# A graph layer on one core: edge blocks taken in pairs, b_e added by TensorE for 20 blocks, the last chunks in parts

## The chip, the cores and the metric

The kernel runs on 1 core of one Trainium2 chip. The metric is the device time of one execution in microseconds (us). Before the change it was 1358.65 us, the median of 3 runs (1356.51 to 1364.21). Times inside an execution come from one profiled execution, counted from the start of its span.

## What is computed

One layer of a graph network on 8192 nodes of 256 features and 131072 edges of 64 features, all in float32. The edges are sorted by their target node `dst`.

```python
ea = edge_attr @ w_e + b_e                              # 131072 x 256
msg = relu(x[src] + ea)                                 # rows of x gathered by src
agg = segment_sum(msg, dst, num_segments=8192)
t = x + agg
h_local = bn1(relu(t @ w1 + b1) @ w2 + b2 + x)
h_attn = bn2(attention(x in groups of 32 nodes, 4 heads) @ out_w.T + out_b + x)
out = h_local + h_attn
out = bn3(out + relu(out @ m_w1 + m_b1) @ m_w2 + m_b2)
return layernorm(x + out)
```

The three `bn` are a scale and a shift for each feature. The rows `x[src]` lie anywhere in x, so each edge fetches its own row of 1 KB.

## The kernel before, in words

**Edges.** The edges are cut into 128 blocks of 1024. A block is 4 pieces (NH) of 256 edges, and its 8 tiles of 128 edges have one edge on each partition. For a block the kernel does this:

- `gather` (L117): GpSimd (POOL) issues 8 indirect DMAs, each of which fetches 128 rows of x into the tile `xs`. It has 5 buffers of one block each.
- `load_edges` (L132): SyncE (SP) loads the features of two blocks at a time. `edge_transpose` (L414, L416): TensorE (PE) turns them, ScalarE (ACT) copies the result from PSUM.
- `edge_products` (L428 to L433): TensorE multiplies by w_e with 64 rows of its array at a time, 8 multiplications of 128x256 for a block; VectorE (DVE) adds the gathered rows (L430) and ScalarE applies relu in place (L433). The message tile `msg` has 2 buffers.
- `edge_sums` (L440 to L454): since the edges are sorted, each piece of 256 edges reaches at most 32 neighbouring target nodes (WN). A one-hot matrix made by VectorE (L440) sums the messages on TensorE into `pw` (L449), which ScalarE copies to `ws` (L454). `pw` and the turned edges share one PSUM slot.
- `edge_place` (L463 to L478): a second one-hot matrix (L463) and two multiplications (L468) move the sums of a block to their nodes; after each second block VectorE adds the result to the turned x, `xT` (L478).

**b_e.** It is added in one of two ways. For the first NX = 13 blocks the gather reads x itself, and VectorE adds b_e to the messages by a second instruction (L432). For the other blocks the gather reads `xb`, a copy of x + b_e in DRAM. `copy_x` makes that copy during the first blocks: SyncE loads 512 rows of x into `xp` (L491), VectorE adds b_e (L492), SyncE writes them to `xb` (L486). It borrows four buffers of 512 KB from tiles that later stages use.

**Nodes.** The nodes are cut into 16 chunks of 512. For each chunk `attention` and later `dense` run; they are Python generators that issue a piece of TensorE work and then yield an estimate of its time. `dense` of a chunk needs the sums of all its edges.

**The order.** TensorE runs its instructions in the order in which the program issues them. The main loop goes over the blocks. For block b it issues the load of block b+2, the gather of b+2, the products of b, then a third of the node work, the sums of b-1, another third, the turning of b+2, the last third, and the placing of b-2. `Work.run` takes pieces from two streams (attention and dense) in turn, up to an allowance of PER = 4.875 us by the estimates for each block. The other engines' orders are set by a scheduler when the program is built. Each engine waits in its order: an instruction that waits holds up all behind it. SyncE's queue holds its DMAs in the same way.

**Start and end.** Before the loop, a setup turns the index lists and the weights on TensorE, and makes the one-hot offsets on VectorE. At the end the last chunk's `dense` is issued in three parts (nodes 0 to 255, 256 to 383, 384 to 511 of the chunk), one after the other in one stream, since all three use the same buffers.

Of the kernel before, what the change touches and what calls it, by code (L numbers as in the profile page):

```python
# [9 lines left out]
FP = mybir.dt.float32  # L10
# [8 lines left out]
P = 128  # L19
# [17 lines left out]
NX = 13  # L37
ND = 2
AGG_ROWS = N + 2 * P
# [10 lines left out]
def gnn_kernel(ctx: ExitStack, tc: tile.TileContext, x, src, dst, edge_attr, w, out):  # L50
# [7 lines left out]
    nc.sync.dma_start(srcd, src[0 : ND * BE].rearrange("(g p j) -> p g j", p=P, j=TJ))  # L58
# [9 lines left out]
    nc.vector.memset(eps_t, LN_EPS)  # L68

# [37 lines left out]
    npool = fast.enter_context(tc.tile_pool(name="node", bufs=1))  # L107

# [3 lines left out]
    def gather(b):  # L112
        xs = epool.tile([P, NH, TJ, C], FP, name="xs", tag="xs", bufs=5)
# [27 lines left out]
    gather(1)  # L141

    with tc.tile_pool(name="setup", bufs=1) as sp, tc.tile_pool(name="setup_ps", bufs=4, space=PSUM) as sps:


        srci_r = npool.tile([P, BE], I32, name="srci_r", tag="y", bufs=2)
        dsti_r = npool.tile([P, BE], I32, name="dsti_r", tag="y", bufs=2)
        nc.sync.dma_start(srci_r, src.rearrange("(s e) -> s e", s=NB))
        nc.sync.dma_start(dsti_r, dst.rearrange("(s e) -> s e", s=NB))
        nc.scalar.dma_start(be, w["b_e"][None, :].to_broadcast([P, C]))  # L150
        for h in range(2):
            nc.scalar.dma_start(we[h * ED : (h + 1) * ED, :], w["w_e"])
        in_r = npool.tile([P, 3 * KC, C], FP, name="in_r", tag="m1")
        out_r = npool.tile([P, KC, C], FP, name="out_r", tag="h1")
        nc.scalar.dma_start(in_r, w["in_w"].rearrange("(o p) c -> p o c", p=P))
        vec_r = sp.tile([nrows, P], FP, name="vec_r")
        for v in VECS:
            r, n = col[v]
            nc.scalar.dma_start(vec_r[r : r + n, :], w[v].rearrange("(r p) -> r p", p=P))
        nc.scalar.dma_start(out_r, w["out_w"].rearrange("(o p) c -> p o c", p=P))  # L160
        srcf = npool.tile([P, NH, P, TJ], FP, name="srcf", tag="zT")
        nc.vector.tensor_copy(srcf.rearrange("s h p j -> s (h p j)"), srci_r)
        dstf = npool.tile([P, NH, P, TJ], FP, name="dstf", tag="y", bufs=2)
        nc.vector.tensor_copy(dstf.rearrange("s h p j -> s (h p j)"), dsti_r)
        for h in range(NH):
            ps = sps.tile([P, TJ, NB], FP, name="ps", tag="ps")
            for j in range(TJ):
                nc.tensor.transpose(ps[:, j, :], srcf[:, h, :, j], ident)
            nc.vector.tensor_copy(srci[:, :, h * TJ : (h + 1) * TJ].rearrange("p s j -> p j s"), ps)

# [6 lines left out]
        for h in range(NH):  # L177
            ps = sps.tile([P, TJ, NB], FP, name="ps", tag="ps")
# [22 lines left out]
        ps = sps.tile([P, 2, NB], FP, name="ps", tag="ps")  # L201
# [7 lines left out]


        nc.vector.memset(bd, 0.0)
        for rows, cols, no in ((in_r, inT, 3 * KC), (out_r, outT, KC)):
            for o in range(no):
                ps = sps.tile([P, KC, P], FP, name="ps", tag="ps")
                for k in range(KC):
                    nc.tensor.transpose(ps[:, k, :], rows[:, o, k * P : (k + 1) * P], ident)
                nc.scalar.copy(cols[:, :, o * P : (o + 1) * P], ps)
        ps = sps.tile([P, nrows], FP, name="ps", tag="ps")
        nc.tensor.transpose(ps, vec_r, ident[:nrows, :nrows])
        nc.vector.tensor_copy(vec, ps)  # L220

        for s, g in ((s1, "bn1_g"), (s2, "bn2_g"), (s3, "bn3_g")):
            nc.vector.tensor_scalar(s, v_(g, 0, KC), RS, None, ALU.mult)
        nc.vector.tensor_add(s12, s1, s2)
        t1 = sp.tile([P, KC], FP, name="t1")
        t2 = sp.tile([P, KC], FP, name="t2")
        nc.vector.tensor_mul(t1, s1, v_("b2", 0, KC))
        nc.vector.tensor_mul(t2, s2, v_("out_b", 0, KC))
        nc.vector.tensor_add(t1, t1, v_("bn1_b", 0, KC))
        nc.vector.tensor_add(t2, t2, v_("bn2_b", 0, KC))  # L230
        nc.vector.tensor_add(cA, t1, t2)
        t3 = sp.tile([P, KC], FP, name="t3")
        nc.vector.tensor_mul(t3, s3, v_("m_b2", 0, KC))
        nc.vector.tensor_add(c3, t3, v_("bn3_b", 0, KC))


    def attention(n0, st, pool, bank, bank2):
# [24 lines left out]
        for t0 in range(0, TN, 2):  # L262
# [10 lines left out]
            nc.vector.tensor_copy(vn[:, t0 : t0 + 2, :].rearrange("p t c -> p (t c)"), ps)  # L273
            yield 1.7

        pr = pool.tile([P, TN, H, NPG], FP, name="pr", tag="pr")
        for hh in range(H // 2):
# [15 lines left out]
            yield 0.9  # L293
# [16 lines left out]
        for k in range(KC):  # L310
# [12 lines left out]
            yield 0.9  # L323
        for o in range(KC):
# [8 lines left out]
            yield 1.7  # L333

    def dense(n0, st, pool, bank, t_a=0, t_z=TN):

        nt = t_z - t_a
# [11 lines left out]
        h1 = pool.tile([P, KC, CH], FP, name="h1", tag="h1")[:, :, : nt * P]  # L349
# [8 lines left out]
        m1 = pool.tile([P, 2 * KC, CH], FP, name="m1", tag="m1")[:, :, : nt * P]  # L358
# [3 lines left out]
        zT = pool.tile([P, KC, CH], FP, name="zT", tag="zT")[:, :, : nt * P]  # L362
# [10 lines left out]
        y = pool.tile([P, TN, C], FP, name="y", tag="y", bufs=2)[:, :nt, :]  # L373
        st6 = pool.tile([P, TN, 6], FP, name="st", tag="st")
        mv = pool.tile([P, TN, 2], FP, name="mv", tag="mv")
# [12 lines left out]
        rstd = pool.tile([P, TN], FP, name="rstd", tag="rstd")  # L388
# [7 lines left out]
        yield 0.9 * part  # L396


    pps = fast.enter_context(tc.tile_pool(name="fast_ps", bufs=1, space=PSUM))
    chunk = [{} for _ in range(NCH)]  # L400

    def bank():
# [301 lines left out]
```

## Time and profile before

| what | value |
|---|---|
| median of 3 runs | 1358.65 us |
| the profiled execution | 1364.3 us |
| its span, first to last instruction | 1362.5 us |
| TensorE (PE) busy | 1242.5 us, 91% |
| VectorE (DVE) busy | 743.0 us, 55% |
| ScalarE (ACT) busy | 662.5 us, 49% |
| 1024 gathers on GpSimd, busy | 879.3 + 98.7 + 16.5 us |
| DMA, whole span | 206.73 MB, 152 GB/s |

The span leaves out 1.8 us of the profiled execution. Busy is the share of the span in which an engine works on an instruction. A busy share is an average over stages; what sets the end is read from the waits and from the order in time. Durations in the profile are those of single instructions, and TensorE's overlap each other: for the cost of a TensorE step it is better to take the time from its start to the start of the next.

### The profile page before, as it was taken

The numbers are of one execution on the slowest core, as the hardware profiler recorded it, in microseconds if no ns is written. First come the engines' busy times: TensorE is split into PE (matmuls) and PEld (weight loads), VectorE is DVE, ScalarE is ACT, GpSimd is POOL, SyncE is SP. The second block draws the span as 40 slices with busy tenths as digits, with TensorE's granted clock in tenths as the row PEclk, the third lists the DMA queues.
The fourth block names the chain that finished last, engine by engine and source line by source line (L and its number), as shares of the span: only waits on it lengthen the run. The fifth ranks groups of instructions, "written<-read, shape, count | busy, mean of one in ns | idle before, by whom it ended". The sixth has DMA issues, their size and how long they took to land.

```text
span 1362.5 us, 20476 instructions
## 1 busy us (share of the span) xinstructions
PE 1242.5 (91%) x7939; PEld 738.2 (54%) x7939; DVE 743.0 (55%) x1218; ACT 662.5 (49%) x1014; POOL 995.5 (73%) x1032
## 2 busy tenths in 40 slices
PE   2778979899999999999999999999999999999797
PEld 2445545555556555555555555555556565565455
DVE  5687665545556463645546464555645555545452
ACT  1444444545555564545546465454645455554332
POOL 6877777777777777777777777777777777777740
PEclk9889989899999999999999999999999999999899
DMA  8994445445454454545454454544545454454421
GB/s 283 361 352 116 130 117 160 141 136 153 135 169 137 126 161 136 167 136 152 136 148 138 137 165 137 151 136 140 162 123 167 135 164 123 137 148 123 137 62 33
DMA packets 141443, 206.73 MB, mean 152 GB/s; under 512 B 19710, under 2 KB 103964, under 8 KB 141340
## 3 DMA queue, kind: packets, MB, share of 16 engines
q0 software_dynamic: 49152, 134.28, 34.6%
q1 hardware_dynamic: 90768, 69.75, 16.0%
q10 hardware_dynamic: 1420, 1.33, 0.3%
q8 instruction: 64, 1.05, 0.3%
q14 instruction: 39, 0.32, 0.1%
HBM read 188.51 MB, written 16.78 MB: 151 GB/s over the span
## 4 chain that ended last, share of the span: by engine, by line
PE 43%; POOL 23%; issue 12%; DVE 8%; DMA 8%; ACT 5%; SPq 0%; DVEq 0%; POOLq 0%; ACTq 0%
POOL xs L117 23%; PE at L344 15%; PE pe L428 8%; DMA xs<-xb,srci 6%; PE pw L449 4%; PE at L256 4%; DVE msg L430 3%; PE l L468 3%; PE at L266 2%; PE at L327 2%; PE tp L414 2%; ACT msg L433 2%; PE at L315 1%; DVE bd L307 1%; ACT pr L292 1%
## 5 line engine op out<-in xcount | busy, mean ns | idle before, releaser
L117 POOL DMA_INDIRECT xs<-xb,srci x920 | 879.3, 956 | 280.3 <-issue 264.5
L433 ACT ACTIVATE msg<-msg 128x1024 f32<-128x1024 f32 x256 | 269.4, 1056 | 361.1 <-DVE msg L430 309.7
L430 DVE TENSOR_TENSOR msg<-pe,xs 128x1024 f32<-128x1024 f32 x256 | 303.5, 1219 | 62.6 <-PE pe L428 44.0
L428 PE MATMUL pe<-we,eaT 64*128 64x256 f32 x2048 | 263.8, 397 | 1.1 <-ACT pr L292 0.8
L428 PEld LDWEIGHTS pe<-we,eaT 64*128 64x128 f32 x2048 | 190.6, 191 | 46.7 <-issue 20.2
L449 PE MATMUL pw<-msg,oh 128*32 128x256 f32 x2048 | 139.1, 390 | 0.0
L344 PE MATMUL at<-hA,mw 128*128 128x512 f32 (+2 forms) x288 | 127.8, 567 | 5.8 <-DVE hA L354 5.4
L256 PE MATMUL at<-xT,inT 128*128 128x512 f32 x256 | 126.0, 615 | 5.9 <-DVE y L384 4.0
L344 PE MATMUL at<-m,mw 128*128 128x512 f32 (+2 forms) x288 | 117.9, 554 | 6.6 <-ACT xT L246 6.5
L117 POOL DMA_INDIRECT xs<-in_x_dram,srci x88 | 98.7, 1121 | 26.8 <-issue 26.2
L416 ACT COPY eaT<-tp 128x512 f32<-128x512 f32 x128 | 74.5, 582 | 86.7 <-PE tp L414 86.1
L414 PE MATMUL tp<-ident,ea 128*128 128x128 f32 x512 | 81.4, 282 | 35.4 <-ACT ws L454 32.4
L414 PEld LDWEIGHTS tp<-ident,ea 128*128 128x128 f32 x512 | 60.6, 143 | 92.4 <-ACT ws L454 56.6
L449 PEld LDWEIGHTS pw<-msg,oh 128*32 128x32 f32 x2048 | 54.0, 110 | 100.6 <-issue 45.0
L468 PEld LDWEIGHTS l<-oh,ws 128*128 128x128 f32 x512 | 82.3, 195 | 39.5 <-issue 36.9
L440 DVE TENSOR_TENSOR oh<-iota_n,rel 128x256 f32<-128x256 f32 x128 | 54.1, 423 | 75.7 <-PE pw L449 75.6
L468 PE MATMUL l<-oh,ws 128*128 128x160 f32 x512 | 94.2, 308 | 0.5 <-ACT ws L454 0.5
L369 DVE SCALAR_TENSOR_TENSOR zT<-at,s,zT 128x512 f32<-128x512 f32 (+2 forms) x36 | 24.9, 692 | 123.4 <-PE at L344 122.1
L463 DVE TENSOR_SCALAR oh<-iota_n,wrow 128x160 f32<-128x160 f32 x128 | 41.6, 325 | 84.9 <-PE l L468 84.8
L344 PEld LDWEIGHTS at<-m,mw 128*128 128x128 f32 x288 | 49.9, 190 | 57.9 <-issue 45.8
L478 DVE TENSOR_TENSOR xT<-l,xT 128x352 f32<-128x352 f32 (+3 forms) x95 | 42.2, 464 | 62.6 <-PE l L468 62.4
L344 PEld LDWEIGHTS at<-hA,mw 128*128 128x128 f32 x288 | 47.5, 190 | 50.4 <-issue 34.1
(106 smaller groups left out, 1313.8 us busy)
## 6 DMA issues: line engine op xcount, KB each, us to landing
ea<-in_edge_attr_dram SPq DMA_DIRECT2D x64, 512.0 KB, 4.5
xs<-xb,srci POOLq DMA_INDIRECT x920
xn<-in_x_dram SPq DMA_DIRECT2D x16, 512.0 KB, 5.0
xp<-in_x_dram SPq DMA_DIRECT2D x16, 512.0 KB, 6.5
xb<-xp SPq DMA_DIRECT2D x16, 512.0 KB
out_dram<-y SPq DMA_DIRECT2D x15, 512.0 KB, 3.2
xs<-in_x_dram,srci POOLq DMA_INDIRECT x88
mw<-in_L_gnn_m_w_dram SPq DMA_DIRECT2D x2, 512.0 KB
```

Of the source, the lines that this page charges most:

```text
L117: nc.gpsimd.indirect_dma_start(out=xs[:, h, j, :], out_offset=None, in_=x if b < NX else xb[:, :], in_offset=bass.IndirectOffsetOnAxis(ap= ...
L256: nc.tensor.matmul(ps, inT[:, k, o * P : (o + 1) * P], xT[:, k, :], start=(k == 0), stop=(k == KC - 1))
L344: nc.tensor.matmul(ps, wt[:, k, o * P : (o + 1) * P], act[:, k, :], start=(k == 0), stop=(k == nk - 1))
L414: nc.tensor.transpose(tp[:, h, :], ea[:, h, :], ident)
L416: nc.scalar.copy(eaT, tp)
L428: nc.tensor.matmul(pe[:, i, u, :], eaT[rows, h + u, :], we[rows, :], start=True, stop=True)
L430: nc.vector.tensor_add(half, pe, xs[:, h : h + 2].rearrange("p u i c -> p i u c"))
L433: nc.scalar.activation(msg[:, h : h + 2], msg[:, h : h + 2], AF.Relu)
L440: nc.vector.tensor_tensor(oh, iota_n[:, None, :WN].to_broadcast([P, TB, WN]), rel[:, b, :, None].to_broadcast([P, TB, WN]), ALU.is_equal,)
L449: nc.tensor.matmul(pw[h * WN : (h + 1) * WN, :], oh[:, h * TJ + j, :], msg[:, h, j, :], start=(j == 0), stop=(j == TJ - 1),)
L468: nc.tensor.matmul(l2[:, k, odd * NPB : odd * NPB + WB], ws[:, k * P : (k + 1) * P], oh2, start=(not odd and k == 0), stop=bool(odd or alo ...
L478: nc.vector.tensor_add(xT, l2[:, :, a - n : z - n], xT)
```

## The change

The blocks are taken by pairs up to block 117 and one by one for the last 10 (NS). For a pair (b, b+1) the program issues: the products of b, the sums of the pair before (both blocks), the products of b+1, half of the pair's node work, the one-hot matrices of the pair, the turning of b+2, the placing of the pair before, the turning of b+3, the other half of the node work.

- b_e is added on TensorE for the first 20 blocks (NX), by as many multiplications again as the products: the rows of `sel` that pick one row of `be`. VectorE's second add is gone.
- `copy_x` moves 256 rows at a time (XH) through two buffers of its own, and is called for 16 blocks instead of 8; the add of b_e stands just ahead of the write.
- `xs` has 4 buffers instead of 5, `msg` 3 instead of 2.
- The setup turns the edges of blocks 0 and 1 first, then the source indices and the weights, then the target indices; the small vectors are loaded on SyncE's queue. It uses the loop's PSUM buffers.
- `dense` of the last two chunks is issued in parts (two of chunk 14, three of chunk 15), each as soon as its sums are placed; three of the parts use buffers of the attention stage (OTHER) and run in the other stream. In the last 10 blocks the allowance of node work is 1.3 times as large.

```diff
-NX = 13
+NX = 20
+NS = 10
+XH = 256
...
-        xs = epool.tile([P, NH, TJ, C], FP, name="xs", tag="xs", bufs=5)
+        xs = epool.tile([P, NH, TJ, C], FP, name="xs", tag="xs", bufs=4)
...
-            nc.scalar.dma_start(vec_r[r : r + n, :], w[v].rearrange("(r p) -> r p", p=P))
+            nc.sync.dma_start(vec_r[r : r + n, :], w[v].rearrange("(r p) -> r p", p=P))
...
-            half = msg[:, h : h + 2].rearrange("p u i c -> p i u c")
-            nc.vector.tensor_add(half, pe, xs[:, h : h + 2].rearrange("p u i c -> p i u c"))
             if b < NX:
-                nc.vector.tensor_add(half, half, be[:, None, None, :].to_broadcast([P, 2, 2, C]))
-            nc.scalar.activation(msg[:, h : h + 2], msg[:, h : h + 2], AF.Relu)
+                for u in range(2):
+                    for i in range(2):
+                        rows = slice(i * ED, (i + 1) * ED)
+                        nc.tensor.matmul(
+                            pe[:, i, u, :], sel[rows, :], be[rows, :], start=False, stop=True, skip_group_check=True
+                        )
+            n = 2 if b < NB - 1 else 1
+            for u in range(0, 2, n):
+                hs = slice(h + u, h + u + n)
+                nc.vector.tensor_add(
+                    msg[:, hs].rearrange("p u i c -> p i u c"), pe[:, :, u : u + n, :],
+                    xs[:, hs].rearrange("p u i c -> p i u c"),
+                )
+                nc.scalar.activation(msg[:, hs], msg[:, hs], AF.Relu)
...
+        for c in range(k * i - k, k * i):
+            if 0 <= c < N // XH:
+                xp = xp_of.pop(c)
+                nc.vector.tensor_add(xp, xp, be[:, None, :].to_broadcast([P, XH // P, C]))
+                nc.sync.dma_start(xb[c * XH : (c + 1) * XH, :].rearrange("(p t) c -> p t c", p=P), xp)
+        for c in range(k * i, k * i + k):
+            if c < N // XH:
+                xp = xp_of[c] = epool.tile([P, XH // P, C], FP, name="xp", tag="xp", bufs=2)
+                nc.sync.dma_start(xp, x[c * XH : (c + 1) * XH, :].rearrange("(p t) c -> p t c", p=P))
...
+    parts = [
+        (NCH - 2, 0, 2, OTHER), (NCH - 2, 2, 4, None), (NCH - 1, 0, 2, OTHER), (NCH - 1, 2, 3, None),
+        (NCH - 1, 3, 4, OTHER),
+    ]
...
+            edge_products(b)
+            sums = edge_sums(waiting) if waiting else None
+            waiting = list(blocks)
+            if n == 2:
+                edge_products(b + 1)
+            work.run(n * per / 2)
+            if n == 2:
+                copy_x(b + 1)
+            for i in blocks:
+                edge_hot(i)
+            for i in blocks:
+                if i + 2 < NB:
+                    edge_transpose(i + 2)
+                if sums:
+                    place(sums)
+                    sums = None
+            if b < NB - 1:
+                work.run(n * per / 2)
+            b += n
+        work.run(2.0)
+        sums = edge_sums(waiting)
+        work.run(1.0)
+        place(sums)
         work.finish()
```

## The prediction

> **What bounds the kernel now.** I read the page first (busy shares, granted clock, the costly groups), then the waits, then GpSimd's gathers by stretches of time, then the timeline near block 12 and at the end.
>
> ```profile
> PE 1242.5 (91%) x7939; PEld 738.2 (54%) x7939; DVE 743.0 (55%) x1218; ACT 662.5 (49%) x1014; POOL 995.5 (73%) x1032
> ...
> L117 POOL DMA_INDIRECT xs<-xb,srci x920 | 879.3, 956 | 280.3 <-issue 264.5
> ...
> out_dram<-y SPq DMA_DIRECT2D x15, 512.0 KB, 3.2
> ```
>
> ```profile
> POOL xs L117 <- issue: 295.2, 969, 0.3
> ```
>
> ```profile
> 50.00:100.00 50.00, 40.11 (x33) 0.90 1.02 363
> ...
> 500.00:600.00 100.00, 75.77 (x80) 1.00 0.49 142
> ```
>
> The page alone says TensorE, at 91%. The waits correct it: GpSimd's idle time is 0.3 us of issue ahead of nearly every gather, never longer. So its 73% are a full queue: a gather takes 0.947 + 0.303 = 1.25 us, 80 per 100 us, 10.0 us a block (the second stretch above; the columns are GpSimd's busy time and count, clock, DMA share, GB/s). From 50 to 100 us there are only 33 in 50 us, while the DMA engines are saturated by the copy of x (share 1.02).
>
> ```profile
> 6.16 1.10 POOL L117 DMA_INDIRECT xs<-in_x_dram,srcd  x1 [4.56 <-DMA srcd<-in_src_dram]
> ...
> 188.34 1.23 DVE L430 TENSOR_TENSOR msg<-pe,xs 128x1024 f32<-128x1024 f32 x1 [0.17 <-PE pe L428]
> ...
> 1311.40 0.95 POOL L117 DMA_INDIRECT xs<-xb,srci  x1 [0.30 <-issue]
> ```
>
> The gathers run from 6.2 to 1312.4 us: 1306 us, of which 1024 x 1.25 = 1280 are the floor and 26 are slow gathers early on. The add at 188.34 belongs to block 12, whose gathers were issued by 152.8: TensorE runs some 35 us behind GpSimd there, and catches up to about 4 us by the end. So the time is: 6 (start) + 1280 + 26 + 50 after the last gather = 1362.5.
>
> ```profile
> 1347.41 1.39 PE L344 MATMUL at<-xT,w 128*128 128x128 f32 x8
> ...
> 1357.54 0.41 DVE L392 TENSOR_SCALAR y<-y,mv,rstd 128x256 f32<-128x256 f32 x1
> ```
>
> This is the last of the three parts of chunk 15 that run one after the other, 10.5 us by itself.
>
> **The change part by part.** Only three terms can move: the start, what GpSimd loses against its floor (26 us now), and the 50 us behind it.
>
> *Parts at the end.* Now the sums of block 127 start at 1326.9, 7 us after its last relu, behind older node work, and the third part starts 20 us later still, behind the other two. After: in the last 10 blocks TensorE may do 1.3 x 4.875 = 6.3 us of estimated node work per block; the estimates add up to 630 us in all and the allowances to 638, so only what has to wait for the last sums remains. Counted from the last gather: the adds of block 127 end at +5; its sums follow behind the last piece at +10, placing at +12, the add to xT at +13; the part of 128 nodes 10.5 as above, and 2 for the other part that interleaves with it, gives +25.5; from the last VectorE instruction to the end of the span 4.5 (1362.5 - 1358.0). Sum 30 instead of 50: **-20**. Bounds: -14 (blocks of 11 us of TensorE work leave it 6 us behind) to -24.
>
> *b_e on TensorE.* The same multiplications as the products; start to start those take 1.93 us:
>
> ```profile
> 1297.16 2.00 PE L428 MATMUL pe<-we,eaT 64*128 64x256 f32 x16
> 1299.09 1.98 PE L344 MATMUL at<-hA,mw 128*128 128x512 f32 x4
> ```
>
> 20 blocks x 1.93 = 39 us more on TensorE. What goes is VectorE's 26 second adds of 1.22 (32 us), which were off the path except that relu waited for them. From 197 to 1132 us TensorE is busy 901 us for 96 blocks, 9.4 a block. So blocks 8 to 19 need 9.4 + 1.9 = 11.3 where GpSimd needs 10: it falls back further.
>
> *Four xs buffers.* The gather of block g+4 must wait until the adds of block g are done. On GpSimd's floor the gather of block g+4 starts at 6 + 10(g+4). With five buffers TensorE's lag of 35 us never held GpSimd (no such wait in the list); with four, a lag over 30 us does, and what is lost is not won back, since GpSimd has no slack. So GpSimd's loss is the largest value of (end of block g's adds) - 46 - 10g. Slow gathers ahead of that point are absorbed by it, not added: the 26 now go.
>
> *The copy through two small buffers.* This sets when block 8 is added. In the changed program's order of instructions all 32 adds of b_e to `xp` stand on VectorE ahead of block 8's first add to messages. Each has to wait for a load, and each load for the write two tiles before: 16 rounds of load, add, write, one after the other. Behind a waiting `xp` add stand VectorE's message adds, and TensorE behind those for its PSUM; behind the waiting load on SyncE's queue stand the edge loads. The trace has no 256 KB round through one buffer. Nearest rows: a 256 KB write lands in 2.1 us (the DMA list's row of one such output), a 256 KB load in the crowded start in 4.9 (`out_r`), 512 KB loads in 4.5 to 5.0 and writes in 3.2. Lower end: load 2.6 (half of 512 KB's moving time saved), add 0.7, issue and wakes 0.5, write 2.1: 5.9. Upper end: load 4.9, two adds, write 3.2, issues: 9.9. The Trainium skill ("DMA: Bandwidth & Descriptors", section Bandwidth) speaks against this edit: batch DMAs to 1 MiB or more, below that the fixed part rules; its fit for the other descriptor path, 2.0 us + bytes/436e3 (section on the anatomy of a DMA), gives 2.6 for each transfer and an estimate of 6.4 for a round. I take **7.0**, nearer to the lower rows since this copy asks 512 KB each way in 7 us, 150 GB/s with 105 for gathers and some 40 for other loads, under the 363 of the saturated stretch; the rule's round would make the end 9 us earlier.
> First xp add at about 31 us (26.4 now; the vectors now stand ahead of it on SyncE's queue), the last at 31 + 15 x 7 = 136, block 8's adds done at 34 + 105 = **139**. Without the copy TensorE would be there at about 120 (products of block 0 at 36 instead of 41, since no xp add stalls the setup; eight blocks of about 10; some idle time), so the copy decides.
>
> *Then* block 20's adds are done at 139 + 12 x 11.3 = 275. GpSimd's loss: 275 - 46 - 200 = **29**, against 26 now: **+3**. With a round of R us it is 15R - 76. By the clock the term could be larger: from 100 to 200 us the granted clock is 0.91 now, and the skill ("TensorE: Matmul & The Clock Gate", Part 1) says that an idle window of about 3.4 us halves the clock. By that row 12 blocks could cost 10 us more; by the rule, TensorE without such idle windows runs at full speed, as at 400 to 600 us here (1.00). I take the rule's case, because from block 8 on TensorE has work waiting.
>
> *Pairs.* Fewer waits for the shared PSUM slot (TensorE's turning waits 32 us in all for `ws` now). After block 20 TensorE needs 9.4 a block or less against 10.0, so nothing of this reaches the end: worth **0**, hidden by GpSimd. If pairs made TensorE slower than 10.0, each 0.1 would cost 11 us over 108 blocks. I see no such wait: sums, placing and transposes each have other work between them and what they need, and the third msg buffer covers the pair.
>
> *Setup.* First gather at 6 as now; the source indices must be turned by 26 us, when the 16 gathers that need no turning are issued; now that is at 16.7, and a second edge load ahead of them adds 2: **0**. If late by 5, it is absorbed by the loss at block 20.
>
> Sum: 1362.5 - 20 + 3 - 1 (rounding of the terms) = 1344.5 for the span; the profiled execution, 1364.3, would be 1346. It lies 5.6 above the median of the runs; 1358.65 - 18 gives **1341**.
>
> **The rivals.**
> - *The copy is slower* (R of 9 or more, with the loads queueing behind writes on SyncE): loss 15 x 9 - 76 = 59, +33 - 20 = +13: 1372. This is the slower case. It decides from R = 8.7 (+27.6 - 20 = over +6.8). For it: two buffers, strict order on two queues, DMAs 4 times longer in the crowded stretch (11.2 at most). Against it: the rows of 2.1 and 3.2.
> - *Nothing measurable*: R of 7.8 to 8.7, or the late start of the last parts eats the gain: 1358.
> - *The copy hardly holds* (R = 6): block 8 at 124, loss 14, -12 - 20: 1327. For it: the lower rows.
> - *Pairs stall TensorE*: 10.2 a block after block 20 gives +22, 1363; against it 9.4.
>
> **How the numbers follow.** About 0.5% is what a measurement of this kernel can tell from no change: 6.8 us. The likeliest, 1341: 0.42; the quick copy, 1327: 0.22; nothing measurable, 0.17; the slow copy 0.13 and stalls of the pairs 0.06 end slower or just above no change. Faster 0.64, same 0.18, slower 0.18. The range: R = 6 with the best end (-36) gives 1322, taken down to 1319 for the start; above, R = 8.7 with the weak end (-14) is +13.6, 1366 with something taken off for both together. The likeliest case's own range is 1330 to 1351.
>
> **What would show it.** In the profile after: the gathers' first wait for `msg` adds (four buffers), and where; the last xp add near 136 and block 8's adds near 139; the last gather near 1315; 30 us behind it. Wrong would be: gathers that are held after block 20, an end behind the last gather of over 40 us, or a granted clock of 0.9 from 140 to 280 us.

## The result, and the profile after

The changed kernel takes 1405.01 us (median of 4 runs, 1400.7 to 1409.8); the kernel before takes 1358.2 (median of 4). Ratio 1.034, 95% interval 1.029 to 1.039: slower by about 46 us, where 18 faster was forecast. The profiled execution took 1402.89 us, its span is 1401.1, against 1362.5 before.

The page after, with the rows that answer to those of before:

```profile
PE 1259.7 (90%) x8307; PEld 791.2 (56%) x8307; DVE 711.8 (51%) x1222; ACT 667.6 (48%) x966; POOL 981.4 (70%) x1032
...
L134 POOL DMA_INDIRECT xs<-xb,srci x864 | 824.1, 954 | 267.9 <-issue 249.5
...
L134 POOL DMA_INDIRECT xs<-in_x_dram,srci x144 | 140.0, 972 | 84.4 <-DVE msg L465 42.9
...
out_dram<-y SPq DMA_DIRECT2D x14, 512.0 KB
```

TensorE's share is 90% where it was 91%, so busy shares tell nothing. What is new is the idle time before the gathers of the first blocks: 42.9 us of it end with an addition to messages. The waits after:

```profile
POOL xs L134 <- issue: 293.0, 962, 0.3
...
DVE xp L527 <- DMA xp<-in_x_dram: 67.3, 26, 6.4
...
POOL xs L134 <- DVE msg L465: 51.9, 22, 14.4
...
PE at L384 <- DVE hA L394: 28.0, 8, 4.5
```

Three waits are new or much longer: GpSimd for free xs buffers (51.9 us, as four buffers made one expect), VectorE for the loads of the copy (67.3; 15.7 before), and TensorE for a vector step inside `dense` (28.0; 5.4 before). Where the time lies is seen when the span is cut at the first product of blocks 20 and 118 (L451 in the timeline after, L428 before):

| stretch | before, us | after, us | difference |
|---|---|---|---|
| start to block 20 | 261.8 | 287.4 | +25.6 |
| block 20 to block 118 | 962.4 | 976.7 | +14.3 |
| block 118 to the end | 138.3 | 137.0 | -1.3 |
| span | 1362.5 | 1401.1 | +38.6 |

The last gather ends at 1340.4 us, 60.7 ahead of the end (before: 1312.3 and 50.2), and the last additions to messages come 36.2 us behind it (before 6.4): at the end GpSimd no longer sets the pace, TensorE is late. From the last additions to the end it is 24.5 us.

**The first stretch.** TensorE from the first product of block 0 to that of block 20, first before, then after (columns: length, busy time and count of PE, PEld, DVE, ACT, POOL, then clock, DMA share, GB/s):

```profile
40.80:261.80 221.00, 186.02 (x1225) 115.25 (x1224) 147.57 (x194) 99.68 (x157) 171.12 (x163) 0.92 0.61 192
```

```profile
31.10:287.40 256.30, 212.97 (x1497) 145.00 (x1496) 117.24 (x178) 97.41 (x141) 162.47 (x170) 0.92 0.60 182
```

TensorE is busy 27.0 us longer and idle 43.3 us in place of 35.0; the first product comes 9.7 us sooner. 27.0 + 8.3 - 9.7 = 25.6. What TensorE's idle time waits for shows on VectorE, here in the changed kernel from 48 to 72 us:

```profile
48.88 0.69 DVE L527 TENSOR_TENSOR xp<-xp,be 128x512 f32<-128x512 f32 x1 [4.89 <-DMA xp<-in_x_dram]
50.86 0.69 DVE L527 TENSOR_TENSOR xp<-xp,be 128x512 f32<-128x512 f32 x1 [1.28 <-DMA xp<-in_x_dram]
56.94 0.69 DVE L527 TENSOR_TENSOR xp<-xp,be 128x512 f32<-128x512 f32 x1 [5.38 <-DMA xp<-in_x_dram]
61.54 0.69 DVE L527 TENSOR_TENSOR xp<-xp,be 128x512 f32<-128x512 f32 x1 [3.91 <-DMA xp<-in_x_dram]
62.15 1.28 DVE L310 COPY vn<-at 128x512 f32<-128x512 f32 x2
68.08 0.69 DVE L527 TENSOR_TENSOR xp<-xp,be 128x512 f32<-128x512 f32 x1 [4.65 <-DMA xp<-in_x_dram]
69.61 0.69 DVE L527 TENSOR_TENSOR xp<-xp,be 128x512 f32<-128x512 f32 x1 [0.84 <-DMA xp<-in_x_dram]
70.22 2.35 DVE L465 TENSOR_TENSOR msg<-pe,xs 128x1024 f32<-128x1024 f32 x2
```

VectorE spends these 21 us on six additions of the copy, each of which waits for its load; the next additions to messages start at 70.22.

**The second stretch.** The same 400 us before and after:

```profile
851.00:1251.00 400.00, 379.55 (x2452) 221.16 (x2450) 211.83 (x351) 207.03 (x310) 303.31 (x318) 1.00 0.50 143
```

```profile
851.00:1251.00 400.00, 360.74 (x2328) 216.06 (x2324) 201.84 (x339) 198.12 (x274) 303.45 (x318) 0.96 0.49 142
```

GpSimd issues 318 gathers in both. TensorE does less after (2328 instructions in place of 2452), is idle 39 us in place of 20, and its clock is 0.96 in place of 1.00. Two of the gaps on TensorE, then VectorE ahead of the second:

```profile
1032.30 2.84 PE L384 MATMUL at<-hA,mw 128*128 128x512 f32 x6 [3.29 <-DVE hA L394]
...
1107.42 1.99 PE L384 MATMUL at<-h,w 128*128 128x512 f32 x4
1109.24 1.02 PE L384 MATMUL at<-hA,mw 128*128 128x512 f32 x2
1113.54 5.49 PE L384 MATMUL at<-hA,mw 128*128 128x512 f32 x6 [3.29 <-DVE hA L394]
```

```profile
1109.04 1.22 DVE L465 TENSOR_TENSOR msg<-pe,xs 128x1024 f32<-128x1024 f32 x1
1110.18 0.69 DVE L345 STREAM_TRANSPOSE bd<-pr 32x512 f32<-32x512 f32 x1
1110.80 1.17 DVE L465 TENSOR_TENSOR msg<-pe,xs 128x1024 f32<-128x1024 f32 x1
1112.00 0.70 DVE L345 STREAM_TRANSPOSE bd<-pr 32x512 f32<-32x512 f32 x1
1112.74 0.75 DVE L394 SCALAR_TENSOR_TENSOR hA<-at,s,hA 128x512 f32<-128x512 f32 x1
```

At the second gap the layer of w2 (h by w) ends at 1109.4; the layer of m_w1 (hA by mw), which reads its result, is issued right behind it, with no edge work between. VectorE's update of hA stands behind messages and transposes of the softmax and starts at 1112.74. TensorE idles 3.29 us, and the six multiplications behind the gap take 5.49 us. Behind the first gap, of the same length and kind, the same six took 2.84 us; the last section comes back to this. Between 849 and 1264 us such waits for hA come 5 times (18.5 us of the 39.3 us of idle time there).

### The profile page after: what moved, and what is told of

Same layout as the page of the kernel before. It is cut to its first block, busy times and chain, and to the rows that moved or that the text cites. A ratio compares the mean times of both kernels' runs of the same rounds, so it can differ in the third digit from the quotient of the medians.

```text
span 1401.1 us, 21219 instructions
## 1 busy us (share of the span) xinstructions
PE 1259.7 (90%) x8307; PEld 791.2 (56%) x8307; DVE 711.8 (51%) x1222; ACT 667.6 (48%) x966; POOL 981.4 (70%) x1032
## 4 chain that ended last, share of the span: by engine, by line
PE 42%; POOL 19%; DMA 12%; issue 10%; DVE 10%; ACT 6%; DVEq 0%; ACTq 0%; POOLq 0%; SPq 0%
POOL xs L134 19%; PE at L384 14%; PE pe L451 8%; DMA xs<-xb,srci 4%; DVE msg L465 4%; PE pw L489 4%; PE at L293 4%; DMA xb<-xp 3%; DMA xp<-in_x_dram 3%; PE l L507 3%; PE at L365 2%; PE tp L167 2%; PE at L303 2%; DVE bd L345 1%; ACT pr L330 1%
## 5 line engine op out<-in xcount | busy, mean ns | idle before, releaser
L134 POOL DMA_INDIRECT xs<-xb,srci x864 | 824.1, 954 | 267.9 <-issue 249.5
L469 ACT ACTIVATE msg<-msg 128x1024 f32<-128x1024 f32 (+1 forms) x258 | 270.5, 1049 | 356.9 <-DVE msg L465 351.2
L465 DVE TENSOR_TENSOR msg<-pe,xs 128x1024 f32<-128x1024 f32 (+1 forms) x258 | 304.2, 1209 | 112.5 <-PE pe L451 76.8
L451 PE MATMUL pe<-we,eaT 64*128 64x256 f32 x2048 | 265.2, 394 | 23.9 <-DVE msg L465 18.8
L451 PEld LDWEIGHTS pe<-we,eaT 64*128 64x128 f32 x2048 | 188.7, 189 | 108.2 <-issue 39.7
L134 POOL DMA_INDIRECT xs<-in_x_dram,srci x144 | 140.0, 972 | 84.4 <-DVE msg L465 42.9
L293 PE MATMUL at<-xT,inT 128*128 128x512 f32 x256 | 124.6, 627 | 10.4 <-ACT qk L296 3.8
L489 PE MATMUL pw<-msg,oh 128*32 128x256 f32 x2048 | 125.0, 383 | 0.0
L517 DVE TENSOR_TENSOR xT<-l,xT 128x352 f32<-128x352 f32 (+4 forms) x99 | 43.3, 463 | 142.2 <-PE l L507 141.9
L384 PEld LDWEIGHTS at<-hA,mw 128*128 128x128 f32 x304 | 54.9, 199 | 92.4 <-issue 41.5
L507 PE MATMUL l<-oh,ws 128*128 128x160 f32 x512 | 84.6, 308 | 1.1 <-ACT ws L495 1.1
L293 PEld LDWEIGHTS at<-xT,inT 128*128 128x128 f32 x256 | 47.3, 198 | 64.9 <-issue 42.6
L365 PE MATMUL at<-oT,outT 128*128 128x512 f32 x128 | 63.6, 622 | 10.2 <-ACT oT L360 7.8
```

What stands on the lines that cost most here:

```text
L134: nc.gpsimd.indirect_dma_start(out=xs[:, h, j, :], out_offset=None, in_=x if b < NX else xb[:, :], in_offset=bass.IndirectOffsetOnAxis(ap= ...
L293: nc.tensor.matmul(ps, inT[:, k, o * P : (o + 1) * P], xT[:, k, :], start=(k == 0), stop=(k == KC - 1))
L365: nc.tensor.matmul(ps, outT[:, k, o * P : (o + 1) * P], oT[:, k, :], start=(k == 0), stop=(k == KC - 1))
L384: nc.tensor.matmul(ps, wt[:, k, o * P : (o + 1) * P], act[:, k, :], start=(k == 0), stop=(k == nk - 1))
L451: nc.tensor.matmul(pe[:, i, u, :], eaT[rows, h + u, :], we[rows, :], start=(b >= NX or u == 0), stop=(b >= NX), skip_group_check=True,)
L465: nc.vector.tensor_add(msg[:, hs].rearrange("p u i c -> p i u c"), pe[:, :, u : u + n, :], xs[:, hs].rearrange("p u i c -> p i u c"),)
```

## The experiments

Each row cuts the span of the profiled execution as above, in us; the ratio is of run times, each to the kernel before that ran beside it. "e9_no_be", "e9_no_copy_add" and "e8_data" leave out or change part of the computation.

| kernel | to 20 | 20 to 118 | 118 to end | span | ratio to before (95%) |
|---|---|---|---|---|---|
| before | 261.8 | 962.4 | 138.3 | 1362.5 | 1 |
| after | 287.4 | 976.7 | 137.0 | 1401.1 | 1.034 (1.029 to 1.039) |
| e1_copy4 | 279.1 | 977.9 | 137.1 | 1394.1 | 1.024 (1.022 to 1.026) |
| e2_be_vector | 251.9 | 988.5 | 139.1 | 1379.5 | 1.013 (1.011 to 1.015) |
| e9_no_be | 251.8 | 980.0 | 139.8 | 1371.6 | 1.009 (1.005 to 1.013) |
| e9_no_copy_add | 269.9 | 976.7 | 137.0 | 1383.6 | 1.020 (1.016 to 1.023) |
| e9_single4 | 292.0 | 965.5 | 132.7 | 1390.2 | 1.023 (1.020 to 1.027) |
| e3_phase | 292.2 | 1004.2 | 127.1 | 1423.5 | 1.044 (1.042 to 1.046) |
| e5_single | 286.3 | 963.4 | 136.7 | 1386.4 | 1.022 (1.019 to 1.026) |
| e8_hold | 288.5 | 963.0 | 134.6 | 1386.1 | 1.021 (1.017 to 1.024) |
| e8_data | 286.2 | 969.7 | 136.4 | 1392.3 | 1.025 (1.020 to 1.029) |
| e4_allow1 | 286.1 | 977.8 | 129.4 | 1393.3 | 1.028 (1.023 to 1.033) |
| e7_before_parts | 263.8 | 962.6 | 130.6 | 1357.0 | 0.994 (0.993 to 0.996) |
| e10_parts_order | 263.3 | 962.2 | 130.4 | 1355.9 | 0.996 (0.995 to 0.997) |
| e12_be_rest | 256.7 | 970.1 | 135.8 | 1362.6 | 1.002 (1.001 to 1.003) |
| e12_be_rest_single | 253.2 | 972.7 | 130.9 | 1356.8 | 0.996 (0.994 to 0.998) |

### The front: the copy, or b_e on TensorE?

**e1_copy4**, the changed kernel with four copy buffers, two of them borrowed from `dense`:

```diff
-                xp = xp_of[c] = epool.tile([P, XH // P, C], FP, name="xp", tag="xp", bufs=2)
+                tag = ("xp", "h1", "xp", "zT")[c % 4] if c < 22 else "xp"
...
```

> The changed kernel with four buffers for the copy of x instead of two (two of them borrowed from the dense stage until tile 22). Theory that the rounds of the copy set the early stage and TensorE then paces the rest: the last xp add falls from 153 to about 115, the products of block 20 start at about 255 to 265 instead of 287, and the end moves by as much, to a span of about 1375. Rival, that GpSimd's gathers set the end and TensorE is only late: the last gather moves from 1340 to about 1315 and the end moves by the same 25 us, but only if TensorE's lag at the end stays 33 us. If the copy is not the cause, the products of block 20 stay at 287 and the span at 1401.

The last xp addition came at 125.7 us in place of 152.8, so a round took 6.4 us in place of 8.2. But block 8's first product came only 8 us sooner (146.2 for 154.0), and the end 7 us sooner. The pace of the copy alone does not set the front. (The edit also moved the copy's additions further ahead in VectorE's queue: all 32 stand ahead of block 6's additions to messages, in the changed kernel ahead of block 8's.)

**e2_be_vector**, b_e by VectorE's second addition again, without the products with `sel`:

```diff
-                            pe[:, i, u, :], sel[rows, :], be[rows, :], start=False, stop=True, skip_group_check=True
...
+                if b < NX:
+                    half = msg[:, hs].rearrange("p u i c -> p i u c")
+                    nc.vector.tensor_add(half, half, be[:, None, None, :].to_broadcast([P, 2, n, C]))
```

> The changed kernel with b_e added by VectorE's second add for the 20 blocks, as the kernel before did it for 13, and no b_e multiplications. TensorE has 39 us less to do in blocks 0 to 19. If the copy holds those blocks until block 8, only 12 x 1.9 = 23 us of them can show: products of block 20 at about 265 instead of 287, span about 1380. If the b_e multiplications are all hidden behind the copy, 287 and 1401 stay. If VectorE's extra 40 x 1.2 us stands in the way of the copy's adds, block 8 gets later than 154.

Block 20 came at 251.9 us, 35.5 sooner; 21.6 of that were left at the end of the span. The copy was not quicker: its last addition came at 200.3, because the scheduler now put copy additions further back in VectorE's queue (18 of the 32 ahead of block 8's additions to messages). So this run moves two things at once; the next two were made to part them.

**e9_no_be**, no b_e in the first 20 blocks at all (those messages lack it):

```diff
-                            pe[:, i, u, :], sel[rows, :], be[rows, :], start=False, stop=True, skip_group_check=True
...
```

> The changed kernel without any b_e in the messages of the first 20 blocks (no products with the selection matrix; those messages lack b_e, so the output isn't the reference's); the copy with b_e for the later blocks stays. Theory A (the delay of 25.6 us at block 20 against the kernel before is the price of the 16 extra products a block, about 1.9 us each block of TensorE): block 8's first product comes at 139 us in place of 154, block 20's at 250 to 255 in place of 287. Rival B (the copy's additions, which wait for their loads in VectorE's queue with the message additions behind them, set the first eight blocks, whatever TensorE has to do): block 8 stays within 5 us of 154, and block 20 comes at 262 to 268.

Block 20 at 251.8, the same as with 40 additions more on VectorE: at block 20 b_e on VectorE costs nothing, and taking it off TensorE saves 35.6 us. The row for this stretch:

```profile
31.70:251.80 220.10, 178.76 (x1178) 111.67 (x1177) 114.50 (x178) 96.42 (x141) 161.35 (x166) 0.93 0.68 208
```

TensorE is busy 178.8 us in place of 213.0, a difference of 34.2, and idle 41.3 in place of 43.3. It looks as if the added work was paid and nothing else changed. Cut at block 8 it looks otherwise, first the changed kernel, then e9_no_be:

```profile
31.10:154.00 122.90, 86.25 (x577) 60.49 (x577) 52.66 (x75) 37.98 (x58) 70.14 (x73) 0.83 0.76 238
154.00:287.40 133.40, 126.72 (x921) 84.50 (x920) 64.58 (x105) 59.43 (x83) 92.33 (x98) 1.00 0.45 130
```

```profile
31.70:117.40 85.70, 64.31 (x449) 41.90 (x448) 43.06 (x60) 37.46 (x58) 65.29 (x68) 0.94 0.84 260
117.40:251.80 134.40, 114.45 (x730) 69.78 (x729) 71.45 (x119) 58.97 (x83) 96.06 (x99) 0.92 0.58 175
```

The whole difference lies ahead of block 8, where the changed kernel takes 37.2 us longer: TensorE is busy 22 us more, at a clock of 0.83 in place of 0.94, and idle 15 us more. Behind block 8 both take the same time: there the products add 12 us of busy time, and the idle time is 13 us less (6.7 for 20.0). So the two idle times agree by chance. This run does not part the two things either: the copy's additions moved here too (23 of the 32 stand ahead of block 8's additions, and the last came at 170.7 in place of 152.8). How much of the 37 us is the price of the products, and how much comes from that order, stays open. Block 8's time of 117 us lies below both theories.

**e9_no_copy_add**, the copy without its additions (messages from block 20 on lack b_e), the products with `sel` kept:

```diff
-                nc.vector.tensor_add(xp, xp, be[:, None, :].to_broadcast([P, XH // P, C]))
```

> The changed kernel without the additions of b_e in the copy: each half chunk of x is loaded and written on as it is (messages from block 20 on lack b_e, so the output isn't the reference's). The DMAs are the same; VectorE's queue no longer holds 32 additions that wait for loads (67.3 us of waits). Theory A (TensorE's extra products set the front): block 8 within 6 us of 154 us, block 20 within 6 us of 287. Rival B (message additions stuck behind the copy's additions set the first eight blocks): block 8 at 120 to 130 us, block 20 at 255 to 262.

Block 8 came at 111.1 us, 43 sooner: message additions stuck behind copy additions did hold the first blocks, as B said (its times, 120 to 130 and 255 to 262, were both missed). TensorE had the products to do here and still came to block 8 earlier than in e9_no_be. But of the 43 us only 17.5 were left at block 20. TensorE, and below it SyncE's queue:

```profile
121.05 1.03 PE L459 MATMUL pe<-be,sel 64*128 64x256 f32 x8
146.27 1.09 PE L167 MATMUL tp<-ident,ea 128*128 128x128 f32 x4 [24.19 <-DMA ea<-in_edge_attr_dram]
```

```profile
99.71 0.43 SPq L149 DMA_DIRECT2D ea<-in_edge_attr_dram  x1
...
127.65 2.46 SPq L527 DMA_DIRECT2D xb<-xp  x2
131.08 2.21 SPq L531 DMA_DIRECT2D xp<-in_x_dram  x2
134.93 2.85 SPq L527 DMA_DIRECT2D xb<-xp  x2
138.61 0.33 SPq L531 DMA_DIRECT2D xp<-in_x_dram  x1
138.99 0.45 SPq L149 DMA_DIRECT2D ea<-in_edge_attr_dram  x1
```

The next edge load stands behind the copy's loads and writes on SyncE, leaves at 138.99, and TensorE waits 24.19 us for it. One queue was freed, and the other that the copy runs through took over.

**e9_single4**, single blocks from block 4 on:

```diff
-            n = 2 if b < NB - NS else 1
+            n = 2 if b < 4 else 1
...
-            per = PER if n == 2 else 1.3 * PER
+            per = PER if b < NB - NS else 1.3 * PER
```

> The changed kernel with pairs only for the first 4 blocks and single blocks from there, so that beside the run with singles from block 20 on it tells what pairs do between blocks 4 and 20. If pairs are no part of the delay at the front: block 20's first product within 5 us of the 286 us of that run, span 1386 within 6. If two blocks' products ahead of each other's additions do hold TensorE there: block 20 at 265 to 275 and the span 10 us or more below 1386.

Block 20 at 292.0, 5.7 us later than in e5_single (below), which has pairs there. Pairs are not what costs at the front.

### The middle: why TensorE is slow behind block 78

From block 78 to 118 a block takes 10.38 us after and 9.92 before, where the gathers ask for 10.0; between 20 and 78 the changed kernel took 9.68, as it caught up with the gathers.

**e3_phase**, a slightly larger allowance of node work, which shifts the pieces against the blocks:

```diff
-    PER = 39.0 / BPC
+    PER = 39.4 / BPC
```

> The changed kernel with one number different: the allowance of node work for 8 blocks is 39.4 instead of 39.0 us, just the sum of the estimates of one chunk, so that the pieces keep the place against the pairs that they have at blocks 20 to 50. Theory that the pieces drift until two dependent pieces of the dense stage stand next to each other without cover: TensorE's time per block from 78 to 118 falls from 10.4 to about 9.7 us, the lag at the end falls by 25 us, the span to about 1376. Rival, that pairs become slow late for another reason (GpSimd's gathers arriving just in time, contention): 10.4 stays and the span stays within 5 us of 1401.

My direction was wrong: the stretch grew by 27.5 us, and blocks 40 to 60 took 10.29 us each instead of 9.42. TensorE's idle time moved to other neighbours (34.6 us of waits for ScalarE's `h`, 30.1 for its `qk`). What it shows is that TensorE's rate depends on which pieces come to lie side by side.

**e5_single**, pairs only up to block 20 (the allowance as in e9_single4):

```diff
-            n = 2 if b < NB - NS else 1
+            n = 2 if b < 20 else 1
```

> The changed kernel with pairs only up to block 20 and single blocks behind it, so that one block's sums, and runs of node work half as long, stand between the products. Theory A (what slows TensorE behind block 78 is node work in long runs, in which a layer follows at once on the layer whose output VectorE has yet to write): the gaps ahead of m_w1's products (28.0 us in all in the changed kernel, 8 of them) fall to 15 or less, the rate between blocks 78 and 118 goes from 10.4 us a block to 9.8, and the span falls by 15 to 25 us, to about 1380. Rival B (the sums and products of two blocks in one visit are not to blame, and what was lost ahead of block 20 is simply carried to the end): the rate stays at 10.4 and the span within 6 us of 1401.

963.4 us for the stretch, 13 less; the waits of m_w1 on hA fell from 28.0 to 14.3, and the rate from 78 to 118 came to 9.88. Single blocks have runs of node work half as long. This speaks for A, but pairs and long runs went together here.

**e8_hold**, pairs kept, and a rest between w2's and m_w1's layers:

```diff
+HOLD = LATER - 1
...
+        yield HOLD
         m1 = pool.tile([P, 2 * KC, nt * P], FP, name="m1", tag=own[1])
...
+                elif t == HOLD:
+                    self.rest[ready[0]] = 1
```

> The changed kernel, in which a dense stage that has issued its w2 layer rests until the next run of node work, so that m_w1's products never follow at once on the w2 products on which VectorE's update of hA still has to be made. Nothing else is changed. Theory A (that adjacency costs 18.5 us of idle TensorE between blocks 78 and 118, and more through the halved clock behind each gap): the waits of m_w1's products on hA fall from 28.0 us to under 8, the rate from 78 to 118 from 10.4 to 9.8 us a block, the last adds' lag behind the gathers from 36 to about 15 us, the span to about 1380. Rival B (the gaps only stand in for work that is late anyway; another wait takes their place): the gaps go, the rate stays above 10.2 and the span within 6 us of 1401.

963.0 us, 13.7 less, with pairs kept. No wait of m_w1 on hA is left in the list, the rate from 78 to 118 is 10.0, the pace of the gathers. The row of the same 400 us:

```profile
851.00:1251.00 400.00, 369.17 (x2421) 223.13 (x2420) 209.87 (x348) 205.88 (x289) 303.25 (x318) 0.98 0.49 143
```

The clock is at 0.98 in place of 0.96, and 93 TensorE instructions more are done. The last additions came 13.7 us behind the last gather in place of 36.2. So what A forecast for the waits and the lag came, and the rate came to the gathers' pace. My 1380 was too low by 6: the work left behind the last additions grew by 7 (31.9 for 24.5). One thing is not excluded: the rest also shifts all later pieces, and a mere shift moved this stretch by 27.5 us in e3_phase. A rest at another place was not run.

**e8_data**, m_w1's products on another tile that is long ready (the MLP's input is left out of the sum):

```diff
-            nc.scalar.activation(m1[:, o, :], layer(mw1, KC, o, hA), AF.Relu, bias=v_("m_b1", o))
+            nc.scalar.activation(m1[:, o, :], layer(mw1, KC, o, tT), AF.Relu, bias=v_("m_b1", o))
```

> The changed kernel with m_w1's products reading the x tile in place of hA: the same products in the same order, but the output isn't the reference's, as the MLP's input is left out of the sum. No product waits any more for VectorE's update of hA. Theory A: as with the rest between the layers, the waits on hA at m_w1 go (28.0 us to 0), the rate from block 78 to 118 comes to 9.8 us a block or less, and the span to about 1375 to 1385. Rival B (another wait takes the gaps' place): rate above 10.2, span within 6 us of 1401.

Only half came: 969.7 us, and 10.22 a block from 78 to 118. Of the waits for the same step of VectorE 11.5 us were left (4 times). The code gives the likely reason: the layers write into PSUM tiles `at`, of which there are two, and the second output of m_w1 needs the one that the update of hA has yet to read. In the trace m_w1 runs four multiplications ahead of its wait, where the changed kernel runs two, and then waits for L394 (2.43 us at 1108.00). So the edit took the data away and left the buffer; my "no product waits any more" was wrong, and this run tests less than it was meant to. Products of q and k also waited longer for VectorE's `y` (10.7 us, up to 3.7 each, all between blocks 20 and 78), as B would have it.

### The end: parts and allowance

**e7_before_parts**, the kernel before with the parts, the second set of buffers and the allowance of 1.3 in the last 10 blocks:

```diff
+            per = PER if b < NB - NS else 1.3 * PER
...
+                    d = dense(c * CH, chunk[c], npool, bank, t_a, t_z, *([own] if own else []))
+                    work.add(0 if own else 1, d)
```

> The kernel before with one part of the change alone: the last two chunks' dense stage in five parts on two buffer sets and two streams, and 1.3 times the node work in the last 10 blocks. No pairs, b_e and copy as before, five xs buffers. If the parts are worth what was forecast, the last gather stays at 1312 and what lies behind it falls from 50 to about 30 us: span about 1342, 1.5% faster than before. If the larger allowance makes TensorE fall behind GpSimd, as it does in the changed kernel (12.0 us a block in the last nine), the lag at block 127 grows from 6 to 15 or more and the span is 1350 to 1362.

A gain of 7.7 us from block 118 on (130.6 for 138.3), 0.6% of the time, where 20 were forecast.

**e4_allow1**, the changed kernel without the larger allowance:

```diff
-            per = PER if n == 2 else 1.3 * PER
+            per = PER
```

> The changed kernel with the ordinary allowance of node work (4.9 us a block, where the change has 6.3) in the last 10 blocks. In the changed kernel those blocks go at 11.9 to 12.2 us each with TensorE about 94% busy. Theory A (a backlog of node work is worked off in these blocks because the larger allowance lets it in): blocks 118 to 127 go at 10.3 or less, so the last product starts some 15 us sooner, but the work left then stands behind the last placement: the stretch after the last adds grows from 24.5 us to 35 to 40, and the end is within 6 us of the changed kernel's 1401 us span. Rival B (the single blocks themselves, not the node work, are slower): blocks 118 to 127 stay at about 12 us and the end doesn't move or gets later by 10.

Blocks 118 to 127 took 9.8 us each in place of 12.0 and the last product came 20 us sooner, but 12 of them came back behind it (41.3 us from the last product's start to the end for 29.4). A was right that this is a trade of one for the other, and low on what stays: 7.8 us of the span, where within 6 was expected (by the ratios, 1.028 and 1.034, the two intervals overlap).

**e10_parts_order**, e7 with 1.5 times the allowance and the last block's sums ahead of the remaining node work:

```diff
-            per = PER if b < NB - NS else 1.3 * PER
+            per = PER if b < NB - NS else (1.5 * PER if b < NB - 1 else 2.0)
...
-            if b < NB:
+            if b < NB - 1:
```

> The kernel before with the last chunks in parts and two buffer sets (1357 us, 0.994 of the kernel before) and two further edits: 7.3 us of node work a block in the last 10 blocks in place of 6.3, and almost none between the last block's products and its sums, so that the sums and the placement of block 127 stand ahead of the work that is left. If the last placement sets the end: it comes at 1324 us in place of 1335, and with 22 us behind it the span is about 1346 to 1350. Rival: TensorE was busy without a gap from 1317 to 1350 us, so the order doesn't matter, only the amount: span within 3 us of 1357.

The rival was right. The last placement came 10.8 us sooner than in e7, the last step of the output only 1.1. First e7, then e10:

```profile
1334.70 0.81 PE L468 MATMUL l<-oh,ws 128*128 128x160 f32 x4 [0.55 <-ACT ws L454]
```

```profile
1352.04 0.41 DVE L392 TENSOR_SCALAR y<-y,mv,rstd 128x256 f32<-128x256 f32 x1
```

```profile
1323.92 0.81 PE L468 MATMUL l<-oh,ws 128*128 128x160 f32 x4 [0.55 <-ACT ws L454]
```

```profile
1350.90 0.41 DVE L392 TENSOR_SCALAR y<-y,mv,rstd 128x256 f32<-128x256 f32 x1
```

Here it is the amount of work left that counts at the end; its order hardly does.

### Both causes away

**e12_be_rest** joins e2 and e8_hold; **e12_be_rest_single** adds single blocks from 20 on. The same two kernels also ran on another chip, where the kernel before took 1916 us: 2004 us (ratio 1.049) and 1902 us (0.992). There the profile has long waits whose cause it cannot name (165 us on ScalarE in the one, 227 in the other), so the argument does not rest on these.

> The changed kernel with b_e by VectorE's second addition in the first 20 blocks and the rest between w2 and m_w1; pairs, half-chunk copies, four xs buffers and parts stay. If the two causes are the whole loss and add up: block 20 at 252 us, the loss of the gathers 33 us in place of 57, the last adds some 14 us behind the last gather, span 1386 - 24 = 1362, to 1357 if TensorE keeps up all the way. If something else in the change still costs: 1370 or more, with a rate above 10.2 us a block somewhere behind block 20. If it beats before's 1358.5 us clearly (under 1352), the parts' gain of about 20 us comes through as I forecast it.

> As the run beside it, with single blocks from block 20 on. If pairs cost something of themselves once the layers no longer adjoin: 8 us or more below that run, about 1350. If they don't: within 5 us of it.

1363.97 us (span 1362.6), as forecast for two causes that add up: the kernel is back at before's time, not below. This is not all that the change costs, though: against e7, which has the new end alone, block 20 comes 7 us sooner, but the middle and the end take 13 us more. Which part of the change costs this is open. With single blocks 1356.27 us, 7.7 less. This is not a better rate in the middle (972.7 for 970.1); it comes 3.5 us ahead of block 20, where the two programs issue the same work, and 4.9 behind block 118. What pairs as such cost stays open at this size, between the 5 and the 8 us that were to decide it; on the other chip the single blocks took 5% less. e12_be_rest_single, e7 and e10 are the only ones below before, by 0.4 to 0.6%, and their intervals do not put one of them first.

## Why the prediction was wrong

Forecast for the span: -20 (parts) + 3 (front) + 0 (pairs). Measured, by the three stretches: -1.3, +25.6, +14.3.

*"The copy decides" block 8, and the loss is +3.* This step failed, in two terms. Block 8's additions to messages end at 162.9 us in the changed kernel, at 131.2 in e9_no_be and at 119.4 in e9_no_copy_add:

```profile
160.54 2.35 DVE L465 TENSOR_TENSOR msg<-pe,xs 128x1024 f32<-128x1024 f32 x2
```

```profile
130.03 1.16 DVE L458 TENSOR_TENSOR msg<-pe,xs 128x1024 f32<-128x1024 f32 x1
```

```profile
117.07 2.36 DVE L465 TENSOR_TENSOR msg<-pe,xs 128x1024 f32<-128x1024 f32 x2
```

The first term is the hold of the copy. Without its additions 119.4 us is what the forecast had (120); with them it was to be 139 and was 162.9, so the hold cost 43 us in place of 19. A round took 8.2 us in place of 7.0 (the rule's estimate of 6.4 was further off), which is 18 of the 24 us; most of the rest is that the additions of block 8 ended 10 us behind the copy's last, not 3. The forecast took its round from loads of 4.5 to 5.0 us of other tiles; the same list of the kernel before has the copy's own loads:

```profile
xp<-in_x_dram SPq DMA_DIRECT2D x16, 512.0 KB, 6.5
```

The second term is the products with `sel`, which were charged nothing ahead of block 8, as hidden behind the copy. Without them block 8's additions ended 31.7 us sooner although the copy was still there. So forecast and kernel differ in kind: the copy's hold and TensorE's work were taken as alternatives of which the later counts, and taking away either one moved block 8 by 32 to 43 us. (In e9_no_be part of this may be the changed order of the copy's additions.) At block 20 the price was 35.6 us.

Behind block 8 the forecast was right: 11.1 us a block for 11.3. Block 20's additions end at 291.0, which makes the loss 291.0 - 46 - 200 = 45 in place of 29. With the measured round, 15R - 76 gives 47, but e1 shows that this agreement is by chance: at R = 6.4 the formula says 20, and 36.6 was measured.

*Four buffers.* The mechanism was right: GpSimd waited for message additions, 51.9 us in all, 12 times for longer than the ordinary 0.3 us of issue, between 73 and 314 us. It hands on TensorE's lateness: with b_e on VectorE (e2) no such wait is longer than 0.3 us. What a fifth buffer would have saved in the changed kernel was not run.

*The clock.* Between blocks 8 and 20 it was right: 1.00 from 154 us on, the rule's case. Ahead of block 8 it was 0.83, which the forecast had not priced, and behind block 78 0.96, through gaps that I had not seen.

*Pairs: "worth 0, hidden by GpSimd... I see no such wait".* This step failed. TensorE's need of 9.4 a block or less was right (busy 9.2 from block 20 to 78, 9.4 from 78 to 118); it was wrong that only work counts. 0.6 us a block of slack has to hold all waits as well: behind block 78 they were 39.3 us, 0.98 a block. The longer runs of node work put w2's layer and m_w1's side by side. The rival "pairs stall TensorE at 10.2", to which I gave 0.06, is what happened behind block 78 at 10.4. Its name was wrong: with the rest (e8_hold) pairs reach 10.0.

*Parts: -20.* This term was mis-sized. The 30 us from the last gather assumed that only the work of the last sums remains. From the last additions to the end the forecast was right (24.5 for 25), but only because TensorE had come late: in blocks 118 to 127 it did the backlog at 12 us a block. With TensorE on time (e7) 37.5 us remain behind the last additions. What was too small is the work that has to wait for the last two chunks; the sum of estimates (630 against 638) does not say when a piece becomes free to be done. The gain was 8 us in e7.

## What to carry to other kernels

When one engine is nearly as full as the one that paces, count its waits with its work: 9.4 us of work in 10.0 leave 0.6 for every wait, and taking off it again the 1.9 us a block of 20 blocks brought back 35.6 us at block 20. When independent work is merged into longer runs, look at which dependent steps become neighbours; a rest of one run between them brought back 14 us here. Before charging a step as hidden, name the idle time that is to hide it, and cut the stretch where the limits change: behind block 8 the run without the products was idle for about as long as they take, ahead of block 8 they came on top of the waits.

## What had not been expected of the hardware

A gap of 3.29 us in TensorE's work can cost more than itself. The clock around the gap that ends at 1113.54, in the changed kernel (it stands behind the counts of the five engines):

```profile
1109.30:1112.70 3.40, 0.96 (x3) 0.13 (x1) 3.37 (x4) 1.75 (x2) 2.52 (x3) 1.00 0.38 108
1112.70:1119.50 6.80, 5.96 (x10) 2.76 (x11) 2.17 (x4) 2.29 (x4) 5.24 (x6) 0.50 0.35 101
1119.50:1125.00 5.50, 5.50 (x23) 3.37 (x22) 1.05 (x3) 2.33 (x5) 4.21 (x5) 0.99 0.63 188
```

The clock halves while the gap still lasts and stays so for 6.8 us. TensorE works 5.96 us of them, so some 3.0 us are lost on top of 3.29 (an estimate: half of 5.96). Length alone does not decide it. Behind the other gap of 3.29 us, which ends at 1032.30, the clock stays at 1.00 and the six multiplications take 2.84 us instead of 5.49; a gap of 2.29 us that ends at 783.91 is followed by 3.4 us at 0.50. By the traces' records of the clock there are 9 such stretches of 3.4 or 6.8 us between blocks 20 and 118 in the changed kernel, 44 us in all, and 2 before, 7 us in all.

The Trainium skill ("TensorE: Matmul & The Clock Gate", Part 1) says this of idle windows of about 3.4 us that run free of the program. The lengths of the stretches agree with that, and a window that runs free of the program would explain why gaps of one length have two outcomes. But the window need not be idle throughout: in the 3.4 us ahead of 1112.7 TensorE still worked 0.96. I had cited the rule for the start and had not looked for such gaps in the steady state.
